# Spreading all parameter tables with TensorE in a conditional residual adapter with layer norm

## The chip, the cores and the metric

The kernel runs on one core of a Trainium2 chip. The core has five engines that run at the same time and wait for each other through semaphores: TensorE (PE, matrix products and transposes into PSUM), VectorE (DVE), ScalarE (ACT), GpSimd (POOL) and SyncE (SP, which here only issues transfers). Weight loads of TensorE are shown as an engine of their own, PEld. Transfers between device memory and the on-chip memory (SBUF) run on sixteen DMA engines.

The metric is the device time of one execution in microseconds (us). Beside it the profile has the span, from the first to the last instruction of one profiled execution.

## The reference

There are 128 batch rows, each a matrix of 128 positions by 512 features, and ten languages. Every batch row has a language, and with it weights and parameters of its own:

```
w1 = W1[language_ids]                       # 512 x 128 for each batch row
w2 = W2[language_ids]                       # 128 x 512
h = relu(einsum('bsh,bha->bsa', x, w1) + b1[language_ids])
adapted = einsum('bsa,bah->bsh', h, w2) + b2[language_ids]
y = x + adapted
normed = (y - mean(y)) * rsqrt(var(y) + 1e-5)
out = x + normed * gamma[language_ids] + beta[language_ids]
```

Mean and variance are taken over the 512 features. All is in float32. The output is 128 x 128 x 512.

## The kernel before

**Tiling.** One batch row is one tile of 128 positions (partitions) by 512 features. Below, "row b" is a batch row, and "row r" or "spread row" is a row of a parameter table. Rows of x come in groups of four (`load_x`, 1 MB; the first twelve rows as pairs, `load_part`), and results leave in pairs (`store`). The language of a row is a number in a register (`lid`), by which the tables are sliced as the kernel runs.

**One row's way.** `transpose_x` turns the four 128 x 128 blocks of x (TensorE, line 238), `copy_xT` takes them out of PSUM (ScalarE, L242), `down` multiplies by W1 (four products, each in two passes, L261), `relu` adds b1 (ScalarE, L269), `up` multiplies by W2 into a PSUM tile `py` (L278). For rows 0 to 3, and for one row in four or eight later, `up` first adds b2 with a product of its own (L277). For the others GpSimd adds b2 to x (`add_b2`, L248), or VectorE does (L291). `residual` (VectorE, L293) adds x or that sum and takes the row sums; `square` (ScalarE, L308), `deviation` and `rstd_1` to `rstd_4` make the reciprocal deviation; `scale` (VectorE, L342) multiplies by gamma; GpSimd has meanwhile made x + beta (`add_beta`, L255); `finish` (VectorE, L351) puts both together and frees the PSUM tile. Five PSUM tiles are shared by all `py` and by the spread rows (pool `p_y`); transposes and products down have one each (`p_x`, `p_h`).

**Order.** The order on every engine is the order of writing: `keep` ties each instruction to the one before it on its engine. The loop over `i` (line 506) runs the stages of several rows, shifted: in step i TensorE transposes row i, multiplies row i - 1 down and row i - 2 up, while VectorE works on row b = i - 3 and older ones. The last five rows have a schedule of their own (`tail`).

**Weights.** The first eight rows have W1 of their language loaded for them alone (`load_first`, tiles `w1s`, five buffers, so that the load for row 5 waits for `down(0)`). From row 8 on ScalarE copies a language's W1 out of a table of all ten (`stage_w1`, L229), at the end of step i for row i + 1, ahead of `copy_xT(i + 1)`. There are two tables. `w1e` is loaded early and used up to `EARLY`; its lines are split over the partitions as `(p k)`, so that x is transposed from every fourth column. `w1` is loaded in four parts within the loop (`load_w1`) and used from row `EARLY` on, with x transposed from neighbouring columns. W2 for all languages is one tile, which every `up` slices by language.

**Parameter tables.** gamma, beta and b2 have ten rows of 512 each, and every partition needs a copy. `rows` holds all thirty rows on partitions of their own; `parts` holds them as three bfloat16 parts, and a product with a column of `pick` spreads one row over the 128 partitions in PSUM (`spread`, L210), from where VectorE or ScalarE copies it into the table (L215, L213). The twenty rows of beta and gamma go this way, in turns between the first products. b2 is loaded a second time as one long line on one partition, into the memory of `w1`, and GpSimd spreads it with three broadcasts (L204):

```
b2_row = w1.rearrange("p l k a -> p (l k a)")[0:1, :]
keep(nc.gpsimd.partition_broadcast(b2_b[:, span], b2_row[:, span]))
```

**Transfers.** All large transfers are issued by SP, in the order of writing: ids, gamma, x of rows 0 and 1, two languages of W2, W1 for rows 0 and 1, x of rows 2 and 3, W1 for rows 2 and 3, the other eight languages of W2 as two transfers, then x and W1 for rows 4 to 7, x of rows 8 and 9, `w1e` in two halves, x of rows 10 and 11. In the loop follow stores, groups of x and the four parts of `w1` (steps 8, 10, 12 and 14). A transfer that has to wait holds up those behind it on SP. ScalarE's queue issues beta, b2, b1 and the b2 line.

The warm-up `spin(11, H)` runs eleven idle products on TensorE first.

Of the kernel before, what the change touches and what calls it, by code (L numbers as in the profile page):

```python
# [17 lines left out]
G = 4  # L18
EPS = 1e-5
FIRST = 8  # L20
EARLY = 28
U = 2


# [1 line left out]
def cond_resid_kernel(ctx: ExitStack, tc: tile.TileContext, x, itok, W1, b1, W2, b2, gamma, beta, out):  # L26
# [8 lines left out]
    nc = tc.nc  # L35
    B, S, H = x.shape
    L, _, A = W1.shape
# [7 lines left out]
    def keep(ins):  # L45

        engine = ins.ins.engine
        if engine in last:
            tc.add_manual_dep(ins.ins, last[engine], behind, reason="kept order")
        last[engine] = ins.ins.name  # L50
        return ins
# [15 lines left out]
    def load_x(g):  # L67
        t = xp.tile([P, G, H], FP, tag="x", name=f"x_{g}")
        keep(nc.sync.dma_start(out=t, in_=x[g * G : (g + 1) * G].rearrange("b s h -> s b h")))
        xs[g] = t  # L70

    def xb(b):
        return xs[b // G][:, b % G, :]
# [5 lines left out]
    w1 = const.tile([P, L, KC, A], FP, name="w1")  # L79
# [13 lines left out]
    load_part(0, 2)  # L93
    keep(nc.scalar.dma_start(out=b1r, in_=b1))

    b2_row = w1.rearrange("p l k a -> p (l k a)")[0:1, :]
    keep(nc.scalar.dma_start(out=b2_row, in_=b2.rearrange("(o l) h -> o (l h)", o=1)))

    warm = const.tile([P, 1], FP, name="warm")
    keep(nc.vector.memset(warm, 1.0))  # L100
    keep(nc.scalar.activation(warm, warm, AF.Sqrt))
    def load_w1(k):
        keep(
            nc.sync.dma_start(out=w1[:, :, k, :], in_=W1[:, k * P : (k + 1) * P, :].rearrange("l p a -> p l a"))
        )
# [10 lines left out]
    R = 3 * L  # L116
# [17 lines left out]
    def lid(b, engine):  # L134
        g = b // G
        if (g, engine) not in lids:
            loads, vals = nc.values_load_multi_w_load_instructions(
                lang[0:1, g * G : (g + 1) * G],
                engines=[engine],
                min_val=0,  # L140
                max_val=L - 1,
                skip_runtime_bounds_check_because="clamped on the chip to 0..L-1 above",
            )
            for ins in loads:
                keep(ins)
            lids[g, engine] = vals
        return lids[g, engine][b % G]
# [4 lines left out]
    def load_first(b):  # L152
        w1s[b] = wp.tile([P, KC, A], FP, tag="w1s", name=f"w1s_{b}")
        src = W1[bass.ds(lid(b, ET.SP), 1)].rearrange("o (p k) a -> p (o k a)", k=KC)
        keep(nc.sync.dma_start(out=w1s[b].rearrange("p k a -> p (k a)"), in_=src))  # L155

    def load_w2(lo, hi):
        dst = w2[:, lo * H : hi * H].rearrange("p (l h) -> p l h", l=hi - lo)
        keep(nc.sync.dma_start(out=dst, in_=W2[lo:hi].rearrange("l a h -> a l h")))  # L159
# [2 lines left out]
        dst = w1e[:, lo:hi].rearrange("p l k a -> p l (k a)")  # L162
        keep(nc.sync.dma_start(out=dst, in_=W1[lo:hi].rearrange("l (p k) a -> p l (k a)", k=KC)))

    load_w2(0, 2)
    load_first(0)
    load_first(1)
    load_part(2, G)
    load_first(2)
    load_first(3)  # L170
    load_w2(2, 6)
    load_w2(6, L)
    xs[1] = xp.tile([P, G, H], FP, tag="x", name="x_1")
    for b in (G, G + 2):
        load_part(b, b + 2)
# [23 lines left out]
    beta_b = const.tile([P, L * H], FP, name="beta_b")  # L199
    gamma_b = const.tile([P, L * H], FP, name="gamma_b")  # L200
    b2_b = const.tile([P, L * H], FP, name="b2_b")
    for l in range(0, L, 4):
        span = slice(l * H, min(l + 4, L) * H)
        keep(nc.gpsimd.partition_broadcast(b2_b[:, span], b2_row[:, span]))  # L204

    def spread(r, copier):
        t = (beta_b, gamma_b)[r // L]
        row = p_y.tile([P, H], FP, tag="y", name=f"row_{r}")
        pick_r = pick[:, r : r + 1].to_broadcast([96, P])
        keep(nc.tensor.matmul(row, lhsT=pick_r, rhs=parts[:96, :], start=True, stop=True))  # L210
        dst = t[:, r % L * H : (r % L + 1) * H]
        if copier is nc.scalar:
            keep(nc.scalar.copy(dst, row))  # L213
        else:
            keep(nc.vector.tensor_copy(dst, row))  # L215
# [10 lines left out]
    def stage_w1(b):  # L226
        w1s[b] = wp.tile([P, KC, A], FP, tag="w1s", name=f"w1s_{b}")
        src = (w1e if b < EARLY else w1).rearrange("p l k a -> p (l k a)")[:, bass.ds(lid(b, ET.Activation) * (KC * A), KC * A)]
        keep(nc.scalar.copy(w1s[b].rearrange("p k a -> p (k a)"), src))  # L229

    def transpose_x(b):
        pxs[b] = p_x.tile([P, KC, P], FP, tag="xT", name=f"pxT_{b}")
        for k in range(KC):
            if b < EARLY:
                cols = xb(b).rearrange("s (p k) -> s k p", k=KC)[:, k, :]
            else:
                cols = xb(b)[:, k * P : (k + 1) * P]
            keep(nc.tensor.transpose(pxs[b][:, k, :], cols, ident))  # L238

    def copy_xT(b):  # L240
        xT[b] = tp.tile([P, KC, P], FP, tag="xT", name=f"xT_{b}")
        keep(nc.scalar.copy(xT[b], pxs.pop(b)))  # L242
# [14 lines left out]
    def down(b):  # L257
        phs[b] = p_h.tile([P, P], FP, tag="h", name=f"ph_{b}")
        for k in range(KC):
            keep(  # L260
                nc.tensor.matmul(  # L261
                    phs[b], lhsT=w1s[b][:, k, :], rhs=xT[b][:, k, :], start=(k == 0), stop=(k == KC - 1)
                )
            )
        del xT[b], w1s[b]

    def relu(b):
        hT[b] = tp.tile([P, P], FP, tag="hT", name=f"hT_{b}", bufs=6)
        keep(nc.scalar.activation(hT[b], phs.pop(b), AF.Relu, bias=b1T[:, bass.ds(lid(b, ET.Activation), 1)]))  # L269

    def up(b):
        v = lid(b, ET.PE)
        ys[b] = p_y.tile([P, H], FP, tag="y", name=f"py_{b}")
        m = b2_by_matmul(b)
        if m:
            pick_b = pick[:, bass.ds(v + 2 * L, 1)].to_broadcast([96, P])
            keep(nc.tensor.matmul(ys[b], lhsT=pick_b, rhs=parts[:96, :], start=True, stop=False))  # L277
        keep(nc.tensor.matmul(ys[b], lhsT=hT[b], rhs=w2[:, bass.ds(v * H, H)], start=not m, stop=True))  # L278
        del hT[b]
# [78 lines left out]
    def on(b):  # L358
        return 0 <= b < B
# [122 lines left out]

    def spread_turn(lo, hi):
        for r in range(lo, hi):
            spread(r, nc.scalar if r % 3 == 1 else nc.vector)

    spread_turn(0, 2)
    transpose_x(0)
    transpose_b1()
    copy_xT(0)  # L490
    spread_turn(2, 6)
    transpose_x(1)
    copy_xT(1)
    spread_turn(6, 10)
    for b in range(4):
        down(b)
        if b < 2:
            transpose_x(b + 2)
        relu(b)
        if b < 2:  # L500
            copy_xT(b + 2)
        spread_turn((10, 14, 18, 20)[b], (14, 18, 20, 20)[b])
    up(0)
    up(1)

    for i in range(3, B + U):
        b = i - U - 1
        if b > G and b % G == 2 and b // G + 3 < NG:
            load_x(b // G + 3)
        if i == 5:  # L510
            load_x(3)
        if i in (8, 10, 12, 14):
            load_w1((i - 8) // 2)
        if i == 4:
            up(2)
        if i == 5:
            up(3)
        if i > 3 and on(i):
            transpose_x(i)
        if b <= E:  # L520
            add_b2(b + 2)
            add_beta(b)
        if i > 4 and on(i - 1):
            down(i - 1)
        if i > 3 and on(i):
            copy_xT(i)
        if i > 4 and on(i - 1):
            relu(i - 1)
        if i > 5 and on(i - U):
            up(i - U)  # L530


        g, half = divmod(b, 2)
        p = g - 1
        mine, old = 0 <= p < B // 2, 0 <= p - 1 < B // 2
        if b == E:
            add_b2(b + 3)
            add_beta(b + 1)
            add_b2(b + 4)
            for n in range(b + 2, B):  # L540
                add_beta(n)
        if b > E:
            tail(b)
        elif half == 0:
            if on(b):
                residual(b)
            if mine:
                rstd_1(p)
                scale(2 * p)
            if on(b):  # L550
                negative_mean(b)
            if mine:
                rstd_2(p)
            if old:
                finish(2 * p - 1)
                store(p - 1)
            if mine:
                rstd_3(p)
        else:
            if on(b):  # L560
                residual(b)
            if mine:
                rstd_4(p)
                scale(2 * p + 1)
            if on(b):
                negative_mean(b)
            if mine:
                finish(2 * p)
        if 0 <= b <= E:
            square(b)  # L570
            if half == 1:
                deviation(g)
        if i + 1 >= FIRST and on(i + 1):
            stage_w1(i + 1)

        for n, engine in ((i + 3, ET.Activation), (i - U + 3, ET.PE), (b + 1, ET.DVE), (b + 5, ET.Pool)):
            if on(n):
                lid(n, engine)
# [37 lines left out]
```

## Time and profile before

| what | value |
|---|---|
| median of three runs | 312.70 us (312.29 to 314.03) |
| profiled execution | 312.74 us |
| its span | 311.0 us |
| mean granted clock of TensorE | 0.989 of full speed |
| TensorE busy | 297.9 us, 96% |
| VectorE busy | 294.7 us, 95% |
| GpSimd busy | 285.4 us, 92% |
| ScalarE busy | 277.8 us, 89% |
| mean transfer rate | 250 GB/s over the span, 218 to 388 GB/s in the first six of forty slices |
| three broadcasts (L204), recorded | 5.6 us, from 10.65 us on |
| one `add_beta` / `add_b2` (L255 / L248), recorded mean | 1.29 us |

Busy shares are averages over the whole span. A TensorE product's end is modelled in the record, so its engine is read here by the starts of successive instructions. Spans on GpSimd are rough in the record. A releaser in brackets is inferred from semaphore events: it is the event that came last before an instruction started.

### The profile page before, as it was taken

What the parts mean: (1) busy time and instruction counts of PE and PEld (TensorE: products, weight loads), DVE (VectorE), ACT (ScalarE), POOL (GpSimd) and SP (SyncE); (2) the same over time, 40 slices, a digit from 0 to 9 for tenths busy, and PEclk for the clock granted to TensorE, in tenths of its full rate; (3) what the DMA queues carried; (4) which work ended last, traced back from release to release, by engine and by line L of the source; (5) the groups of instructions that cost most, each with busy time, mean ns of one, the idle gap of its engine ahead of it and who ended that gap; (6) DMA issues with size and microseconds to landing.
All of it is one profiled execution on the core that took longest, in us unless ns stands there. A gap on an engine that the chain in (4) does not pass through costs nothing.

```text
span 311.0 us, 7063 instructions
## 1 busy us (share of the span) xinstructions
PE 297.9 (96%) x1846; PEld 223.1 (72%) x1846; DVE 294.7 (95%) x941; ACT 277.8 (89%) x710; POOL 285.4 (92%) x237
## 2 busy tenths in 40 slices
PE   8998899999999999999999999999999999999970
PEld 3766677878777777777777777777777777777740
DVE  6845999999999999999999999999999999999995
ACT  2655899999999999999999999999999999999982
POOL 1606999999999999999999999999999999999974
PEclk9999999999999999999999999999999999999995
DMA  6999999876777757677866766577765767773234
GB/s 218 346 387 388 373 368 349 295 263 210 269 271 238 233 192 245 231 237 254 270 245 211 232 201 265 209 266 271 249 227 194 245 233 239 245 270 135 87 154 169
DMA packets 43499, 77.61 MB, mean 250 GB/s; under 512 B 1946, under 2 KB 7077, under 8 KB 43459
## 3 DMA queue, kind: packets, MB, share of 16 engines
q1 hardware_dynamic: 43398, 77.10, 71.8%
q8 instruction: 15, 0.25, 0.3%
q14 instruction: 24, 0.20, 0.2%
q10 hardware_dynamic: 62, 0.07, 0.1%
HBM read 43.60 MB, written 33.55 MB: 248 GB/s over the span
## 4 chain that ended last, share of the span: by engine, by line
PE 83%; DMA 8%; DVE 4%; SPq 1%; issue 1%; ACT 1%; DVEq 1%; POOL 0%; ACTq 0%; POOLq 0%
PE ph L261 33%; PE py L278 32%; PE pxT L238 17%; DMA w1e<-in_L_cond_W_dram 4%; DMA x<-in_x_dram 3%; PE py L277 1%; DVE py L293 1%; DVE py L342 1%; DVE o L351 1%; SPq L155 1%; ACT sq L386 0%; SPq L87 0%; DVEq L611 0%; SPq L159 0%; ACT n L402 0%
## 5 line engine op out<-in xcount | busy, mean ns | idle before, releaser
L255 POOL TENSOR_TENSOR o<-x,beta_b 128x512 f32<-128x512 f32 x128 | 163.2, 1290 | 9.4 <-ACT hT L269 9.4
L261 PE MATMUL ph<-xT,w1s 128*128 128x128 f32 x1024 | 135.5, 275 | 0.0
L278 PE MATMUL py<-w,hT 128*128 x256 | 131.2, 594 | 1.4 <-DVE o L351 1.3
L261 PEld LDWEIGHTS ph<-xT,w1s 128*128 128x128 f32 x1024 | 125.0, 192 | 1.5 <-ACT hT L269 0.8
L248 POOL TENSOR_TENSOR r<-x,b_b 128x512 f32<-128x512 f32 x93 | 120.0, 1291 | 0.0
L238 PEld LDWEIGHTS pxT<-ident,x 128*128 128x128 f32 x512 | 67.4, 154 | 65.4 <-issue 47.3
L342 DVE SCALAR_TENSOR_TENSOR py<-py,nmean,gamma_b 128x512 f32<-128x512 f32 x126 | 93.3, 740 | 0.0
L351 DVE SCALAR_TENSOR_TENSOR o<-py,rstd,o 128x512 f32<-128x512 f32 x122 | 90.7, 744 | 1.4 <-POOL o L255 1.4
L308 ACT ACTIVATE sq<-py,sum 128x512 f32<-128x512 f32 x124 | 84.9, 685 | 4.3 <-DVE py L293 4.3
L238 PE MATMUL pxT<-ident,x 128*128 128x128 f32 x512 | 78.1, 275 | 0.5 <-ACT xT L242 0.5
L242 ACT COPY xT<-pxT 128x512 f32<-128x512 f32 x128 | 75.0, 586 | 1.7 <-PE pxT L238 1.6
L293 DVE SCALAR_TENSOR_TENSOR py<-py,r 128x512 f32<-128x512 f32 x93 | 64.4, 692 | 2.5 <-POOL r L248 1.7
L229 ACT COPY w1s<-w 128x512 f32 x100 | 61.2, 612 | 0.0
L269 ACT ACTIVATE hT<-ph,b1T 128x128 f32<-128x128 f32 x128 | 47.1, 368 | 11.2 <-PE ph L261 7.4
L278 PEld LDWEIGHTS py<-w,hT 128*128 128x128 f32 x256 | 40.4, 192 | 4.7 <-issue 1.7
L293 DVE SCALAR_TENSOR_TENSOR py<-py,x 128x512 f32<-128x512 f32 x35 | 24.3, 695 | 3.3 <-PE py L278 2.7
L308 ACT ACTIVATION_READ_ACCUMULATOR sq<-py,sum 128x1 f32 x124 | 25.2, 203 | 0.0
L319 ACT ACTIVATE sd<-ssq,eps 128x2 f32<-128x2 f32 x62 | 18.3, 296 | 2.1
L299 DVE TENSOR_SCALAR nmean<-sum 128x1 f32<-128x1 f32 x128 | 19.3, 150 | 0.1
L325 DVE RECIPROCAL stat<-sd 128x2 f32<-128x2 f32 x62 | 12.8, 207 | 1.3 <-ACT sd L319 1.3
L204 POOL PARTITION_BROADCAST b_b<-w x3 | 5.6, 1968 | 9.0 <-DVE beta_b L215 9.0
L229 ACT COPY w1s<-w1e 128x512 f32 x20 | 12.2, 612 | 1.3 <-DMA w1e<-in_L_cond_W_dram 1.2
(55 smaller groups left out, 119.7 us busy)
## 6 DMA issues: line engine op xcount, KB each, us to landing
out_dram<-o SPq DMA_DIRECT2D x61, 512.0 KB, 3.6
x<-in_x_dram SPq DMA_DIRECT2D x29, 1024.0 KB, 6.4
x<-in_x_dram SPq DMA_DIRECT2D x6, 512.0 KB, 7.0
w1e<-in_L_cond_W_dram SPq DMA_DIRECT2D x2, 1280.0 KB, 13.4
w<-in_L_cond_W_dram SPq DMA_DIRECT2D x4, 640.0 KB
w1s<-in_L_cond_W_dram SPq DMA_DIRECT2D x8, 256.0 KB, 6.2
w<-in_L_cond_W_dram SPq DMA_DIRECT2D x2, 1024.0 KB
out_dram<-o SPq DMA_DIRECT2D x6, 256.0 KB, 2.0
```

The lines of the kernel that those rows point to most:

```text
L229: keep(nc.scalar.copy(w1s[b].rearrange("p k a -> p (k a)"), src))
L238: keep(nc.tensor.transpose(pxs[b][:, k, :], cols, ident))
L242: keep(nc.scalar.copy(xT[b], pxs.pop(b)))
L248: keep(nc.gpsimd.tensor_tensor(rs[b], xb(b), b2_b[:, bass.ds(v * H, H)], ALU.add))
L255: keep(nc.gpsimd.tensor_tensor(os[g][:, j, :], xb(b), beta_b[:, bass.ds(v * H, H)], ALU.add))
L261: nc.tensor.matmul(phs[b], lhsT=w1s[b][:, k, :], rhs=xT[b][:, k, :], start=(k == 0), stop=(k == KC - 1))
L269: keep(nc.scalar.activation(hT[b], phs.pop(b), AF.Relu, bias=b1T[:, bass.ds(lid(b, ET.Activation), 1)]))
L278: keep(nc.tensor.matmul(ys[b], lhsT=hT[b], rhs=w2[:, bass.ds(v * H, H)], start=not m, stop=True))
L293: nc.vector.scalar_tensor_tensor(ys[b], ys[b], 1.0, r, ALU.mult, ALU.add, accum_out=col(sums, b))
L308: nc.scalar.activation(sq, ys[b], AF.Square, bias=col(sums, b), scale=-float(H), accum_out=col(ssqs, b))
L342: nc.vector.scalar_tensor_tensor(ys[b], ys[b], col(nmeans, b), gamma_b[:, bass.ds(v * H, H)], ALU.add, ALU.mult)
L351: nc.vector.scalar_tensor_tensor(o, ys.pop(b), rstds[g][:, j : j + 1], o, ALU.mult, ALU.add)
```

## The change

The ten rows of b2 are spread by TensorE like those of beta and gamma, so there are thirty rows. The second load of b2, its line in the memory of `w1` and the three broadcasts on GpSimd are gone. The spread rows take other turns between the first transposes and products down: all thirty, and all four products down, now come before the first product up, and the transposes of rows 2 and 3 come after `down(1)`. ScalarE copies three rows of every seven (13 of 30; before, 7 of 20), VectorE the others (17; before, 13).

The first transfer of W2 has three languages in place of two, and the other seven follow as one transfer. `EARLY` is 24 in place of 28, and the four parts of `w1` are issued in steps 12, 14, 16 and 18 in place of 8, 10, 12 and 14.

```diff
-EARLY = 28
+EARLY = 24
...
-    b2_row = w1.rearrange("p l k a -> p (l k a)")[0:1, :]
-    keep(nc.scalar.dma_start(out=b2_row, in_=b2.rearrange("(o l) h -> o (l h)", o=1)))
...
-    load_w2(0, 2)
+    load_w2(0, 3)
     load_first(0)
     load_first(1)
     load_part(2, G)
     load_first(2)
     load_first(3)
-    load_w2(2, 6)
-    load_w2(6, L)
+    load_w2(3, L)
...
-    for l in range(0, L, 4):
-        span = slice(l * H, min(l + 4, L) * H)
-        keep(nc.gpsimd.partition_broadcast(b2_b[:, span], b2_row[:, span]))
 
     def spread(r, copier):
-        t = (beta_b, gamma_b)[r // L]
+        t = (beta_b, gamma_b, b2_b)[r // L]
...
-            spread(r, nc.scalar if r % 3 == 1 else nc.vector)
+            spread(r, nc.scalar if r % 7 in (1, 3, 5) else nc.vector)
+
+    def x_turn(b):
+        transpose_x(b)
+        copy_xT(b)
 
     spread_turn(0, 2)
     transpose_x(0)
     transpose_b1()
     copy_xT(0)
     spread_turn(2, 6)
-    transpose_x(1)
-    copy_xT(1)
-    spread_turn(6, 10)
-    for b in range(4):
-        down(b)
-        if b < 2:
-            transpose_x(b + 2)
-        relu(b)
-        if b < 2:
-            copy_xT(b + 2)
-        spread_turn((10, 14, 18, 20)[b], (14, 18, 20, 20)[b])
+    x_turn(1)
+    spread_turn(6, 11)
+    down(0)
+    relu(0)
+    spread_turn(11, 15)
+    down(1)
+    relu(1)
+    x_turn(2)
+    spread_turn(15, 19)
+    x_turn(3)
+    down(2)
+    relu(2)
+    spread_turn(19, 24)
+    down(3)
+    relu(3)
+    spread_turn(24, R)
     up(0)
     up(1)
...
-        if i in (8, 10, 12, 14):
-            load_w1((i - 8) // 2)
+        if i in (12, 14, 16, 18):
+            load_w1((i - 12) // 2)
```

## The prediction

> **What bounds the kernel now.** I read four views, in this order: the busy sums and the forty slices of the page, the chain that ended last, the waits and order of time of each engine in the first 36 us, and the DMA rate in half-microsecond stretches.
>
> First the sums and the chain of waits (start in us, length in us, what). From 33.36 us on the chain is nothing but TensorE, always transpose, product down, product up; before that it is two transfers, one behind the other.
>
> ```profile
> PE 297.9 (96%) x1846; PEld 223.1 (72%) x1846; DVE 294.7 (95%) x941; ACT 277.8 (89%) x710; POOL 285.4 (92%) x237
> 8.18 10.55 DMA x<-in_x_dram
> 18.74 13.36 DMA w1e<-in_L_cond_W_dram
> 33.36 0.74 PE pxT L238 x4
> 34.10 0.89 PE ph L261 x8
> 34.99 0.86 PE py L278 x2
> 75.44 0.22 PE py L277
> 76.52 0.44 PE pxT L238 x4
> ```
>
> Each batch row costs TensorE 0.47 + 0.89 + 0.86 = 2.22 us up to 76 us and 0.44 + 0.89 + 0.86 = 2.19 after, when the transposed columns no longer lie strided (row 28 on, `EARLY`), plus 0.22 for each b2 product of line 277. The engine never waits between 33.36 us and the last rows. So whatever the change does, its price is read at one point: the start of the ninth row's transpose, T(9), at 33.36. What moves that start moves the end; what happens before it and leaves it alone costs nothing.
>
> Now the front, by engine (start, length, engine, line; in brackets the idle time before and what ended it).
>
> ```profile
> 10.65 5.64 POOL L204 PARTITION_BROADCAST b_b<-w  x3 [8.95 <-DVE beta_b L215]
> 25.69 2.50 POOL L255 TENSOR_TENSOR o<-x,beta_b 128x512 f32<-128x512 f32 x2 [9.39 <-ACT hT L269]
> 26.99 0.75 DVE L351 SCALAR_TENSOR_TENSOR o<-py,rstd,o 128x512 f32<-128x512 f32 x1 [1.40 <-POOL o L255]
> 27.79 0.38 PE L277 MATMUL py<-parts,pick 96*128 96x512 bf16 x1 [0.33 <-DVE o L351]
> 31.72 1.12 PE L278 MATMUL py<-w,hT 128*128 x2 [1.33 <-DVE o L351]
> 32.20 0.62 ACT L229 COPY w1s<-w1e 128x512 f32 x1 [1.18 <-DMA w1e<-in_L_cond_W_dram]
> 33.36 0.74 PE L238 MATMUL pxT<-ident,x 128*128 128x128 f32 x4 [0.52 <-ACT xT L242]
> ```
>
> The reader is to see two separate delays. GpSimd starts its first `add_beta` at 25.69; neither x_0 nor the beta table is that late (its last copy ran at about 11 us), so I take it that the broadcasts hold the engine until then, though their recorded spans end at 16.3. That lateness passes through VectorE's `finish` to TensorE's PSUM buffers: idle at 27.3 to 27.79 and 30.2 to 31.72. Second, w1e lands at 32.10; ScalarE has `stage_w1(8)` ahead of `copy_xT(8)` in its queue, so the copy starts at 32.72 and T(9) at 33.36, 1.26 after the landing, with TensorE idle from 32.58. The second delay ends last.
>
> The transfers run at their limit nearly from the start (us, then busy time of each engine, last the granted clock, DMA share, GB/s):
>
> ```profile
> 7.00:7.50 0.50, 0.50 (x5) 0.38 (x3) 0.20 (x1) 0.50 (x2) 0.00 (x0) 1.00 0.92 160
> 7.50:8.00 0.50, 0.50 (x4) 0.24 (x5) 0.20 (x2) 0.50 (x2) 0.00 (x0) 1.00 0.50 61
> 8.00:8.50 0.50, 0.50 (x4) 0.37 (x3) 0.50 (x1) 0.18 (x2) 0.00 (x0) 1.00 0.92 332
> 20.00:20.50 0.50, 0.50 (x2) 0.20 (x1) 0.35 (x1) 0.23 (x2) 0.00 (x0) 1.00 1.03 381
> ```
>
> **The change part by part.**
>
> *Ten rows more on TensorE.* A spread row costs 0.22 on TensorE (four rows start at 7.54, what follows them at 8.41). Work after the warm-up, from 5.85: first two rows 0.84, 28 rows x 0.2175 = 6.09, first transpose 0.69 and three at 0.47 = 1.41, the b1 transpose 0.16, four products down at 0.89 = 3.57; together 12.76, so `up(0)` starts at 18.61. It starts at 16.96 now. With the copies (next part) I get 18.72; the walk, each step after the one before it: row 10 at 9.75, `down(0)` 9.97, rows 11 to 14 10.86, `down(1)` 11.73, T(2) 12.62, rows 15 to 18 13.09, T(3) 13.96, `down(2)` 14.43, rows 19 to 23 15.32, `down(3)` 16.41, row 24 17.30. But now the first product up waits 0.28 beyond the 0.22 of its b2 row (16.96 to 17.46), because the last of W2 lands about 17.3; at 18.94 it has landed. Two ups then end at 18.72 + 2 x 1.08 = 20.88 against 19.47: TensorE is 1.41 late there.
>
> *Their copies.* Five PSUM buffers: row r waits for the copy of row r-5. VectorE takes 17 copies at 0.62 (three in 1.88) = 10.5 and b1T 0.15, from 6.51, so 17.2 at best; ScalarE 13 at 0.54 (two in 1.08) = 7.0, four xT at 0.55 and four relus at 0.35, 10.6 from 6.94, so 17.6 at best. Both are shorter than TensorE's 18.61. Walking the written order, I find one real hold: row 29 waits for row 24, whose copy stands behind `relu(3)` on ScalarE (17.84 to 18.43); and `up(0)` waits for row 25's, 18.56. Row 28's copy ends at 19.8, ahead of `residual(0)`, which must wait for its product anyway. Bounds: if the copies cost nothing extra, 0; if the ten extra rows went at one engine's pace, 10 x 0.62 = 6.2 in place of 2.17, so +4.0. I take 0.1, because 20 rows went through the same buffers at TensorE's pace with only 0.53 lost (16.96 - 5.85 = 11.11 against 10.58 of work).
>
> *No broadcast on GpSimd.* `add_beta(0)` can run at about 11. `add_b2(4)` waits for row 29 (19.8) and ends at 21.1; `residual(4)`, now kept until 29.45 by it, needs it at about 28. So the two idles of TensorE, 0.50 + 1.50, go. What is late next is w1e. Without any hold, TensorE's work from 19.47 to T(9) is 13.89 - 0.50 - 1.50 - 0.78 = 11.11, so T(9) could start at 20.88 + 11.11 = 31.99. It is held to 33.36 by w1e as now: 1.37 of cover for the ten rows. If that cover were gone (w1e early) the front would decide, and the gain ends there.
>
> [...]
>
> *Loads.* W2's third language (256 KB) comes ahead of the first W1 rows, which land later by 262 KB / 390 GB/s = 0.67; `down(0)` at 9.97 should still find them, since the queue ran empty at about 8.0. One W2 issue (0.5 us of SP) and one 20 KB row go. SP waits for `down(0)`, (1), (2) before the loads of W1 rows 5, 6, 7: by the walk +0.2, -0.5, 0.0; some 2.3 MB stand in the queue at 17.4 (issued 7.4 MB, moved 5.1), 6 us of work, so this is hidden. What counts is whether w1e lands earlier. The bytes ahead of it are the same, so at least 0; at most the whole dip of 7.0 to 8.0 (0.28 MB short of 390 GB/s, 0.72) and 0.05 for the b2 row: 0.77. I take 0.33, the idle DMA share of 7.0 to 8.5 (0.04 + 0.25 + 0.04), because w1e ends with the slowest of the engines and half were still busy in the dip. A late end has no row that speaks for it.
>
> *EARLY 24.* Rows 24 to 27 are transposed from unstrided columns: 4 x (0.47 - 0.44) = -0.12. They read w1, which is loaded four steps later: its last part is issued at about 55 in place of 46, and with 20.8 MB ahead of its end, 12.28 moved by 36 us and 360 GB/s it lands at 59.6. `stage_w1(24)` runs at 67.56; 8 us of cover. In the queue of SP the stores and x loads that stood behind the w1 loads at 32 to 46 us go earlier.
>
> *After T(9).* GpSimd's operations start 1.233 us apart, 14 in eight rows: 17.3 us against TensorE's 17.74, so it is not the bound and an earlier start buys nothing there. The end of the kernel is untouched: GpSimd waits 1.75 us for ScalarE at 300.04.
>
> Sum: -0.33 - 0.12 = -0.45; 312.74 (span 311.0 and 1.74 around it) becomes 312.29. The median of the runs, 312.70, is the same within 0.04; I say 312.3. Half a per cent, 1.6 us, is about what a measurement of this kernel can tell from no change.
>
> [...]
>
> **The rivals.**
>
> *The dip is filled wholly.* w1e lands 0.77 early: 312.74 - 0.77 - 0.12 = 311.85; if other low stretches go too (229 and 176 GB/s at 10.5 to 11.5), TensorE's own order is the floor: 33.36 - 31.99 = 1.37, 311.25. For it: the empty queue. Against: the DMA share of 0.92 in the same stretches.
>
> *The copies set the pace (slower).* ScalarE's queue has relus and xT copies between row copies, each waiting for TensorE, and TensorE waits for the rows behind them. Up to 1.37 us of such waiting is covered; 1.49 makes no gain; 3.05 costs half a per cent. At one engine's pace T(9) starts at 31.99 + 4.03 = 36.02: 312.74 + 2.66 - 0.12 = 315.3. For it: one copy, row 24's, already holds two steps in my walk. Against: the 0.53 above.
>
> *w1 comes late for row 24.* Each us after 67.5 costs one; at 70 us 312.74 + 2.5 = 315.2. Against: 8 us of cover.
>
> *The change doesn't free GpSimd.* If 25.69 was set by ScalarE's relu, as the releaser says, all of GpSimd moves with TensorE by 1.41: `finish(1)` ends at 31.66 + 1.41 = 33.07 and not at 31.66, `up(6)` takes 0.86 behind it, and T(9) starts at about 34.0: 312.74 + 0.64 - 0.12 = 313.3. Against: the first add needs no relu.
>
> **How the numbers follow.** Forecast 0.60 (its own range 311.9 to 312.8); dip filled 0.17; copies 0.12; w1 late 0.05; GpSimd not freed 0.06. Faster by over 0.5% (under 311.1) is only beyond the floor, with the scatter of the runs (0.4 below the median): 0.08. Slower by over 0.5% (above 314.3): half of the copies' case, most of w1's, a part of the last, 0.14. Same 0.78. The range, 311.1 to 314.0, leaves out about 0.07 below and 0.13 above.
>
> **What would show it.** Right: the first `add_beta` near 11 us; no wait of TensorE for `finish` before 32; `up(0)` at 18 to 19; ScalarE still waiting for w1e at `stage_w1(8)`; T(9) at 32.6 to 33.4 and no idle after. Wrong: TensorE waiting for row copies for over 2 us, T(9) after 34, ScalarE waiting for w1 at about 67, or a gain after T(9).

## The result and the profile after

| | before | after |
|---|---|---|
| median, 14 runs each | 312.81 us (312.29 to 314.03) | 311.92 us (311.77 to 312.10) |
| ratio, 95% interval | | 0.9963 (0.9951 to 0.9974) |
| profiled execution, its span | 312.74, 311.0 | 311.92, 310.1 |
| w1e lands | 32.10 | 31.18 |
| ninth transpose, T(9), starts | 33.36 | 32.45 |

By the ratio the kernel is faster by 0.37% (0.26 to 0.49%), which lies within the half per cent that was called no change; the interval keeps clear of no difference. The medians differ by less, 0.89 us or 0.28%: five of the 14 runs of before lie at 313.4 to 314.0, and none of after lies above 312.1. The forecast was 312.3.

The chain of waits of after has the same shape as before: two transfers, then TensorE (start, length, what).

```profile
6.81 10.80 DMA x<-in_x_dram
17.62 13.56 DMA w1e<-in_L_cond_W_dram
31.29 0.08 ACT w1s L222
31.81 0.59 ACT xT L235
32.45 0.74 PE pxT L231 x4
```

The start of the TensorE chain is 0.91 earlier than before. From there the chain runs as before: the product up that started at 75.50 starts at 74.46, 1.04 earlier, the last ones at 298.38 in place of 299.38. The 0.13 between 0.91 and 1.04 belongs to the four rows whose columns no longer lie strided: in the run below that has `EARLY` at 28, the same product starts 42.13 after T(9), in before 42.14, in after 42.01. The profiled time is 0.82 shorter and not 1.0.

The order of time of the engines in the front of after (start, length, engine, line, operation; in brackets the idle time before, and what ended it):

```profile
10.84 2.50 POOL L248 TENSOR_TENSOR o<-x,beta_b 128x512 f32<-128x512 f32 x2 [9.38 <-DVE beta_b L208]
18.87 0.38 PE L270 MATMUL py<-parts,pick 96*128 96x512 bf16 x1 [0.48 <-DVE b_b L208]
19.58 1.26 POOL L241 TENSOR_TENSOR r<-x,b_b 128x512 f32<-128x512 f32 x1 [6.24 <-DVE b_b L208]
28.93 0.38 PE L270 MATMUL py<-parts,pick 96*128 96x512 bf16 x1
31.29 0.62 ACT L222 COPY w1s<-w1e 128x512 f32 x1 [1.12 <-DMA w1e<-in_L_cond_W_dram]
31.37 1.02 PE L271 MATMUL py<-w,hT 128*128 x2
32.45 0.74 PE L231 MATMUL pxT<-ident,x 128*128 128x128 f32 x4
```

GpSimd starts its first `add_beta` at 10.84 and not at 25.69, and TensorE has no wait for `finish` any more (28.93 stood at 27.79 with one, 31.37 at 31.72). TensorE is late at the first product up: 18.87 against 16.96. It makes that good by the missing waits: `up(6)` ends at 32.23, 0.22 before the start of T(9). So ScalarE still waits for w1e and TensorE for ScalarE, but now by 0.22 where it was 0.78.

The transfers, in half microseconds (last the granted clock, the DMA share, GB/s). Of after:

```profile
7.00:7.50 0.50, 0.50 (x4) 0.24 (x5) 0.21 (x2) 0.50 (x2) 0.00 (x0) 1.00 1.07 410
7.50:8.00 0.50, 0.50 (x4) 0.36 (x3) 0.50 (x1) 0.41 (x2) 0.00 (x0) 1.00 1.02 369
11.00:11.50 0.50, 0.50 (x5) 0.47 (x4) 0.50 (x2) 0.50 (x1) 0.50 (x1) 1.00 0.94 369
11.50:12.00 0.50, 0.50 (x7) 0.50 (x7) 0.50 (x2) 0.07 (x1) 0.50 (x1) 1.00 1.02 397
```

And of before, in the second of its low stretches:

```profile
11.00:11.50 0.50, 0.50 (x5) 0.44 (x5) 0.50 (x2) 0.21 (x1) 0.50 (x1) 1.00 0.99 176
11.50:12.00 0.50, 0.50 (x4) 0.19 (x2) 0.16 (x2) 0.39 (x1) 0.50 (x1) 1.00 0.88 295
```

The low stretch at 7 to 8 us is closed, and so is most of the one at 10.5 to 12 (its first half microsecond still has 225 GB/s; before had 229). Summed up, 1.93 MB had moved by 8 us where it was 1.70, and 3.42 MB by 12 us where it was 2.96; a lead of some 0.43 MB is then kept. W1e is complete when 10.8 MB have moved in before, 10.9 in after.

One line of SP's queue differs early on, in before and in after:

```profile
4.73 1.34 SPq L87 DMA_DIRECT2D x<-in_x_dram  x1
```

```profile
4.78 0.42 SPq L87 DMA_DIRECT2D x<-in_x_dram  x1
```

The issue of x for rows 2 and 3 holds SP for 1.34 us in before, though nothing is shown to make it wait, and for 0.42 in after. What follows on SP is earlier by 0.8 to 0.9, and by 1.4 behind the W2 loads (8.18 against 6.81), since one W2 issue of about 0.5 us is gone.

### The profile page after: what moved, and what is told of

Same layout as the page of the kernel before. It is cut to its first block, busy times and chain, and to the rows that moved or that the text cites. A ratio compares the mean times of both kernels' runs of the same rounds, so it can differ in the third digit from the quotient of the medians.

```text
span 310.1 us, 7084 instructions
## 1 busy us (share of the span) xinstructions
PE 298.7 (96%) x1856; PEld 223.5 (72%) x1856; DVE 297.3 (96%) x945; ACT 280.3 (90%) x716; POOL 280.4 (90%) x234
## 4 chain that ended last, share of the span: by engine, by line
PE 83%; DMA 8%; DVE 4%; ACT 1%; issue 1%; SPq 1%; DVEq 1%; ACTq 0%
PE ph L254 33%; PE py L271 32%; PE pxT L231 17%; DMA w1e<-in_L_cond_W_dram 4%; DMA x<-in_x_dram 3%; PE py L270 1%; DVE py L286 1%; DVE py L335 1%; DVE o L344 1%; SPq L152 1%; DMA ids<-in_itok_B_dram 0%; ACT sq L379 0%; DVEq L613 0%; ACT n L395 0%; DVE o L406 0%
## 5 line engine op out<-in xcount | busy, mean ns | idle before, releaser
L231 PEld LDWEIGHTS pxT<-ident,x 128*128 128x128 f32 x512 | 66.7, 152 | 65.0 <-issue 46.4
L222 ACT COPY w1s<-w 128x512 f32 x104 | 63.6, 612 | 0.0
L286 DVE DVE_READ_ACCUMULATOR py<-py,r 128x1 f32 x93 | 13.5, 145 | 0.0
L222 ACT COPY w1s<-w1e 128x512 f32 x16 | 9.8, 611 | 1.1 <-DMA w1e<-in_L_cond_W_dram 1.1
```

The source lines that it names most:

```text
L286: nc.vector.scalar_tensor_tensor(ys[b], ys[b], 1.0, r, ALU.mult, ALU.add, accum_out=col(sums, b))
```

## The experiments

Theory A is that of the prediction: w1e's landing sets T(9), T(9) sets the end, and the ten rows are covered. What the first four runs ask is what made w1e land earlier: the third language of W2 (A), or the b2 line and the broadcasts (B). All ratios are to the kernel before, run beside each kernel; its medians lay at 312.9. Times of events, T(9) above all, are those of the one profiled execution of each kernel.

**The third language in the kernel before.**

```diff
-    load_w2(0, 2)
+    load_w2(0, 3)
...
-    load_w2(2, 6)
+    load_w2(3, 6)
```

> The kernel before with one edit: three languages of W2 ahead of the first W1 rows in place of two. Theory A, the third language closes the low stretch of the transfers at 7 to 8 us: w1e lands at 31.3 to 31.6 and not at 32.1; TensorE still waits for GpSimd, so the ninth transpose starts at 32.6 to 32.8; 0.6 to 0.8 us less than before, about 312.1. Rival B, the removed b2 line and its broadcasts caused the low stretches: w1e lands at 32.1, the issue of x rows 2 and 3 on SP still takes 1.3 us, the time is that of before, 312.8.

Measured: 312.28, ratio 0.9976 (0.9953 to 0.9999). w1e had landed by 31.4. TensorE now waits for GpSimd's lateness, as its own order of time shows:

```profile
28.28 0.38 PE L277 MATMUL py<-parts,pick 96*128 96x512 bf16 x1 [0.91 <-DVE o L351]
32.19 1.12 PE L278 MATMUL py<-w,hT 128*128 x2 [1.31 <-DVE o L351]
33.15 0.63 PE L238 MATMUL pxT<-ident,x 128*128 128x128 f32 x4
```

T(9) starts at 33.15, right behind `up(6)`. So the third language does bring w1e forward by at least 0.7 here. In this execution, which took 312.51, most of that is lost to GpSimd: T(9) is only 0.21 earlier than in before, and misses the expected 32.6 to 32.8. The median of the ten runs (311.65 to 313.67) is lower by 0.64, what theory A expected, so how much is lost in the others isn't shown. SP's hold of 0.9 us is still there, in the pair of W1 issues just before (1.75 in place of 0.91).

**The spreads alone.** The kernel after with the old loads.

```diff
-EARLY = 24
+EARLY = 28
...
-    load_w2(0, 3)
+    load_w2(0, 2)
...
-    load_w2(3, L)
+    load_w2(2, 6)
+    load_w2(6, L)
...
-        if i in (12, 14, 16, 18):
-            load_w1((i - 12) // 2)
+        if i in (8, 10, 12, 14):
+            load_w1((i - 8) // 2)
```

> The kernel after with the old order of loads: W2 as 2, 4 and 4 languages, EARLY 28, the parts of w1 in steps 8 to 14. So only the thirty spread rows and the gone broadcasts and b2 line are new. Theory A (third language): w1e lands at 32.0, the ninth transpose starts at 33.3, the time is that of before within 0.1, 312.7. Rival B (b2 line): w1e lands at 31.2, and the time is 312.05, that of after plus 0.13 for EARLY.

Measured: 312.44, ratio 0.9973 (0.9954 to 0.9992); w1e landed at 31.70, T(9) started at 32.96. That is between the two expectations: 0.4 of the 0.9 comes without any change in the order or size of SP's loads. SP's issue of x took 0.43 here.

**The b2 line back in the kernel after.**

```diff
+    b2_row = w1.rearrange("p l k a -> p (l k a)")[0:1, :]
+    keep(nc.scalar.dma_start(out=b2_row, in_=b2.rearrange("(o l) h -> o (l h)", o=1)))
```

> The kernel after with the second load of b2 put back on ScalarE's queue, one line of 20 KB on one partition, which nothing reads; no broadcasts. Theory A: no change, w1e at 31.2, 311.9. Rival B in the form that the transfer of the line slows the others: w1e at 31.7 to 32.1, the issue of x rows 2 and 3 takes 1.3 us again, 312.4 to 312.8. If the broadcasts themselves slowed the transfers, 311.9 too.

Measured: 311.77, ratio 0.9951 (0.9927 to 0.9974), T(9) at 32.41. The transfer of the line costs nothing that can be seen; SP's issue of x took 0.42.

**Two languages first in the kernel after.**

```diff
-    load_w2(0, 3)
+    load_w2(0, 2)
...
-    load_w2(3, L)
+    load_w2(2, L)
```

> The kernel after with two languages of W2 first and eight in one transfer later. Theory A: the low stretch at 7 to 8 us is back, w1e lands 0.5 to 0.9 later, 312.4 to 312.8. Rival B: w1e at 31.2, 311.9.

Measured: 312.09, ratio 0.9980 (0.9949 to 1.0011; one of ten runs lay at 315.8, with a clock of 0.989, the others at 311.85 to 312.5). w1e landed by 31.2, T(9) started at 32.39. So in the profiled execution, at 311.85 the fastest of the ten, the third language is not needed. The median lies 0.32 above that of the run with the b2 line back, which has the third language and ran on the same chip, so some of its worth may remain. This kernel differs from the spreads alone, where w1e landed at 31.70, in `EARLY`, in the steps of the w1 parts (no w1 load is issued before 31 us in either) and in one thing that comes ahead of w1e: the last eight languages of W2 are one issue on SP and not two. With it x of rows 4 and 5 is issued at 6.50 and not at 7.03, and 7 to 8 us carry 397 and 410 GB/s in place of 320 and 283. The gone issue is thus worth some 0.5 us of w1e's landing in these two executions; the medians differ by 0.35, of which `EARLY` is 0.13. Theory A had the effect right and the cause only half.

**A small broadcast in the kernel after.**

```diff
+    small = const.tile([P, P], FP, name="small")
+    keep(nc.gpsimd.partition_broadcast(small, ident[0:1, :]))
```

> The kernel after with one small broadcast on GpSimd put ahead of its first add_beta: the first line of the identity, 128 columns, into a tile that nothing reads. It brings GpSimd's broadcast code back, not the b2 line and not the 2.6 MB that the three broadcasts wrote. Theory C, formed on the four runs before this one: that the program holds a broadcast at all costs SP about 0.9 us in its issues between 3.8 and 6.1 us, and the low stretch at 7 to 8 us follows; w1e lands at 31.7 to 32.1 and the time is 312.4 to 312.8, with more scatter among the runs. Rival: the low stretches came from the writing of the broadcasts; then 311.9 and SP's issue of x rows 2 and 3 takes 0.42 us.

Measured: 312.01, ratio 0.9957 (0.9933 to 0.9982). Theory C fell: SP's issue took 0.42, w1e landed by 31.0. But GpSimd's order of time shows what a broadcast is:

```profile
1.41 0.30 POOL masks.py:199 TENSOR_SCALAR_AFFINE_SELECT ident<-ident 128x128 f32<-128x128 f32 x1 [0.29 <-POOL ones L109]
10.23 0.43 POOL L199 PARTITION_BROADCAST small<-ident  x1 [8.53 <-DVE beta_b L210]
21.87 2.50 POOL L250 TENSOR_TENSOR o<-x,beta_b 128x512 f32<-128x512 f32 x2 [11.21 <-ACT sq L303]
```

Its input is ready at 1.71 and nothing stands ahead of it on the engine, yet it is recorded at 10.23, and the next add follows at 21.87. With one broadcast of 128 columns GpSimd does nothing else for 20 us. T(9) started at 32.22, at once when `up(6)` ended: an add as late as 21.87 does no harm here.

**One broadcast of three in the kernel before.**

```diff
-    for l in range(0, L, 4):
+    keep(nc.gpsimd.memset(b2_b[:, 4 * H :], 0.0))
+    for l in range(0, 4, 4):
```

> The kernel before with the first of the three broadcasts alone (four languages); the b2 table of the other six is zero, so b2 is left out for them. The question is what holds GpSimd's first add_beta until 25.69. [...] The time stays at 312.8 within its scatter, since w1e still lands at 32.1.

Measured: the first `add_beta` at 23.95, 13.08 after the recorded start of the broadcast; with three it was 15.04 (25.69 - 10.65), with 128 columns 11.64 (21.87 - 10.23). Over 5120 - 128 columns that is 0.68 ns a column, and 11.55 us that do not depend on the size; by this line the 2048 columns would take 12.95. It is an estimate from one execution each: the run with the third language, with three broadcasts too, has 15.23 (26.19 - 10.96). Neither a pure rate by columns (0.4 of the 15.04 after 10.65, 16.67) nor a start set by ScalarE's relu, at about 25.7, met it. What comes ahead of the recorded start is not a fixed amount: 8.5 us with the small broadcast, 6.56 here, behind a memset that ended at 4.31.

The time, 314.36 (a single run), is another matter, and came of the memset in this edit. It kept GpSimd busy from 1.65 to 4.31, and VectorE's two small operations of that time took 2.17 and 2.14 us in place of 0.17 and 0.21:

```profile
2.17 2.17 DVE L123 TENSOR_SCALAR pick<-pick 96x10 bf16<-96x10 bf16 x1
2.25 2.14 DVE L129 TENSOR_SCALAR wrap<-ids 1x128 int32<-1x128 int32 x1
```

The loads behind them came 1.9 us late and w1e landed at 33.7; T(9) started at 34.99, 1.63 later than in before, as the whole time is 1.62 longer. TensorE idled for 1.64 us before its first row (7.68), and from 9.42 to 12.84, by the rows below (0.71 is 0.42 us at full clock, 0.58 is 0.16), its clock was halved (stretch, then busy times, last three: granted clock, DMA share, GB/s):

```profile
8.00:9.00 1.00, 1.00 (x8) 0.78 (x7) 0.76 (x2) 0.69 (x2) 0.00 (x0) 1.00 0.84 236
9.00:10.00 1.00, 1.00 (x5) 0.46 (x4) 0.84 (x3) 0.60 (x2) 0.00 (x0) 0.71 0.93 264
10.00:11.00 1.00, 1.00 (x6) 0.91 (x5) 1.00 (x2) 0.37 (x1) 0.14 (x1) 0.50 0.91 324
11.00:12.00 1.00, 1.00 (x4) 0.30 (x2) 0.65 (x2) 0.67 (x2) 1.00 (x1) 0.50 0.91 318
12.00:13.00 1.00, 1.00 (x5) 0.81 (x4) 0.84 (x3) 0.50 (x1) 1.00 (x1) 0.58 0.88 225
```

The mean clock of this execution is 0.985; that of the profiled execution of before is 0.989, with 1.00 in each hundred microseconds up to 300.

**Without the ten rows.**

```diff
-    b2_b = const.tile([P, L * H], FP, name="b2_b")
+    b2_b = beta_b
...
-        for r in range(lo, hi):
+        for r in range(lo, min(hi, 2 * L)):
```

> The kernel after without its ten last spread rows; add_b2 and VectorE read the beta table in their place, so the b2 table is left out. The question is what the ten rows cost. Theory A (covered by the wait for w1e): up(6) ends 2.2 us earlier, at about 30.1, and the ninth transpose still starts at 32.4: 311.7 to 311.9, at most 0.2 less. Rival D, TensorE's order is the bound: 2.2 less, 309.7.

Measured: T(9) at 32.43, after an idle time of TensorE that is 2.4 us longer; rival D fell.

```profile
28.98 1.02 PE L271 MATMUL py<-w,hT 128*128 x2
32.43 0.75 PE L231 MATMUL pxT<-ident,x 128*128 128x128 f32 x4 [2.42 <-ACT xT L235]
```

The ten runs fell into two groups: five at 311.81 to 312.08, as in after, with a mean granted clock of 0.990 to 0.993, and five at 313.21 to 313.83 with 0.985 to 0.987. Their median, 312.64 (ratio 0.9998, 0.9975 to 1.0021), lies between the groups and says little. So the ten rows cost nothing, and taking them away costs 1.4 us in half of the executions. The profiled execution is one of the first group.

**Ten rows more.**

```diff
     spread_turn(24, R)
+    spread_turn(20, R)
```

> The kernel after with the ten b2 rows spread a second time, ahead of the first product up: forty rows. The cover that is left is 0.2 us (up(6) ends at 32.23, the ninth transpose starts at 32.45). Theory A: ten rows x 0.2175 less 0.2 is 2.0 us more, 313.9. If the copies out of PSUM set the pace for these back-to-back rows, ten rows over two engines at 0.62 and 0.54 are 2.9 us, so up to 314.6; at one engine's pace 318.

Measured: 314.85, ratio 1.0058 (1.0033 to 1.0084). The first product up starts at 22.16 in place of 18.87 and T(9) at 35.52, right behind `up(6)`:

```profile
22.16 0.38 PE L270 MATMUL py<-parts,pick 96*128 96x512 bf16 x1 [0.45 <-DVE b_b L208]
35.52 0.63 PE L231 MATMUL pxT<-ident,x 128*128 128x128 f32 x4
```

Ten rows cost 3.29 us there, 0.33 each and not 0.22, so the copies out of PSUM set their pace; that is nearest to the second form of the expectation (2.9 at two engines), and what is over the cover reaches the end one to one: T(9) +3.07, time +2.9.

**Half a megabyte ahead of w1e.**

```diff
+    more = w1.rearrange("p l k a -> p (l k a)")[:, 0 : 2 * H].rearrange("p (b h) -> p b h", b=2)
+    keep(nc.sync.dma_start(out=more, in_=x[0:2].rearrange("b s h -> s b h")))
     load_early(0, 5)
```

> The kernel after with one transfer more on SP's queue ahead of w1e: x of rows 0 and 1 once more, 512 KB, into the memory of w1, which nothing reads there. Theory A (the end follows w1e one to one): 0.524 MB at 388 GB/s is 1.35 us, w1e lands at 32.5, the ninth transpose starts at 33.8, 313.25, and some runs are slower by a further 1.6, since TensorE then waits 1.5 us. Rival: TensorE's own order is the bound, 311.9.

Measured: 313.20, ratio 0.9998 (0.9980 to 1.0016), 1.28 more than after; ScalarE's copy of w1e started at 32.86 and T(9) at 34.02, each 1.57 later. The profiled execution is 1.47 longer, so the end follows w1e nearly one to one. The further 1.6 us that some runs were expected to lose did not come in ten runs, with an idle time of 1.8 us by the starts (`up(6)` at 31.36, 0.86 long, T(9) at 34.02):

```profile
34.02 0.75 PE L233 MATMUL pxT<-ident,x 128*128 128x128 f32 x4 [1.64 <-ACT xT L237]
```

**The first copy of w1e behind the transpose's copy.** In step 8, on ScalarE:

```diff
             copy_xT(i)
+        if i == FIRST:
+            stage_w1(i)
...
-        if i + 1 >= FIRST and on(i + 1):
+        if i + 1 > FIRST and on(i + 1):
```

> The kernel after with one move on ScalarE: the first stage_w1, of row 8, comes after copy_xT(8) and not ahead of it, so the ninth transpose no longer stands behind w1e. Theory A: w1e needs 0.7 us more until its copy is made (31.9), product down of row 8 wants it at 32.7; the ninth transpose starts when up(6) ends, 32.23 in place of 32.45: 311.7, 0.2 less than after. Rival, w1e binds through the product instead: no change, 311.9.

Measured: 311.58, ratio 0.9947 (0.9929 to 0.9965); nine of eleven runs at 311.53 to 311.79. T(9) starts when `up(6)` ends. The profiled execution is one of the two later ones, 312.29: the transfer of the table rows let `parts` begin at 3.87 and not at 3.08, so that TensorE's whole front came 0.8 late, and with no slack left that reached the end.

**The first product up earlier.** The last edit, and:

```diff
-    spread_turn(24, R)
-    up(0)
+    spread_turn(24, 27)
+    up(0)
+    spread_turn(27, R)
     up(1)
```

> The edit of the last plan (first stage_w1 after copy_xT(8)) and a second one: up(0) comes ahead of the last three spread rows, so that TensorE no longer waits 0.48 us for the copy of row 25 there. W2 landed at 16.2, ahead of it. Theory A: the ninth transpose at about 31.75, product down of row 8 at 32.2, the copy of w1e ready at 31.9: 311.2, 0.7 less than after. Rival: up(0) and up(1) now hold two of the five PSUM tiles while the last rows pass through the others, the wait comes back at rows 28 and 29, and the time is that of the last plan, 311.7.

Measured: 311.43, ratio 0.9949 (0.9924 to 0.9975), eleven of twelve runs at 310.98 to 311.85, one at 315.08 with a clock of 0.991; the median lies between the expected 311.2 and the rival's 311.7. TensorE's wait of 0.48 before `up(0)` is gone, T(9) starts at 31.53:

```profile
17.60 0.38 PE L270 MATMUL py<-parts,pick 96*128 96x512 bf16 x1
31.53 0.63 PE L231 MATMUL pxT<-ident,x 128*128 128x128 f32 x4
34.12 0.75 PE L231 MATMUL pxT<-ident,x 128*128 128x128 f32 x4
```

T(10), at 34.12, is 0.66 ahead of after's 34.78. Its median is the lowest of the kernels that compute everything, but 0.15 below the last plan's is within the scatter. After was not timed on the same chip, so the 0.5 between it and this kernel is a comparison of ratios, 0.9949 and 0.9963, whose intervals overlap.

**The idle time filled.** The kernel without the ten rows, with the product of `up(6)` made three times over, to see whether the second group goes when TensorE's idle time is filled:

```diff
-        keep(nc.tensor.matmul(ys[b], lhsT=hT[b], rhs=w2[:, bass.ds(v * H, H)], start=not m, stop=True))
+        for _ in range(3 if b == 6 else 1):
+            keep(nc.tensor.matmul(ys[b], lhsT=hT[b], rhs=w2[:, bass.ds(v * H, H)], start=not m, stop=True))
```

> The kernel without the ten b2 rows (five of its ten runs were 311.8 to 312.1, five 313.2 to 313.8, these with a mean clock of 0.985 to 0.987 and not 0.990 to 0.993), and up(6) makes its product three times over, each time from the start: 1.7 us more work for TensorE in the 2.4 us in which it waits for w1e. As there, the b2 table is left out. [...]

Measured: 311.87, ratio 0.9949 (0.9929 to 0.9969); ten runs at 311.51 to 312.06, all with a clock of 0.988 or more. With more work on TensorE the second group is gone, 0 of ten runs for five of ten, and the edit changes nothing else. So for that kernel the second group goes with TensorE's idle time. The two kernels ran on different chips, and no execution of the second group was profiled; that its clock was halved for a while is argued from its mean clock alone (0.985 to 0.987 and not 0.990 to 0.993), which is near the 0.985 of the run with one broadcast, where the trace shows the halving, and is not shown: a run of after at 311.84 has 0.987 too.

## Why the prediction was right, and where it was not

**The place and the bound: right.** "Its price is read at one point", T(9): 0.91 there and 0.13 from `EARLY` make up the 1.0 by which TensorE ends earlier, of which the profiled time keeps 0.82. Of the signs that were named, T(9) alone came a little outside, at 32.45 and not 32.6 to 33.4, since w1e was earlier still. The run with 512 KB more ahead of w1e shows that the end follows that transfer; the run without the ten rows shows that TensorE's own work did not decide.

**Ten rows and their copies: right, a little short.** `up(0)` at 18.72 was forecast and came at 18.87, held by row 25's copy as in the walk, for 0.48. `up(6)` ended at 32.23 where 31.99 was worked out as the earliest T(9), so the cover was 1.13 of the 1.37. The ten rows cost nothing in the end. Written back to back, beyond the cover, they would cost 0.33 each: the rival "the copies set the pace" has its mechanism and was 0.22 us away from counting.

**GpSimd: right.** The broadcasts did hold it: 10.84 for the forecast "about 11", and both idles of TensorE are gone. The forecast did not know that most of the price does not depend on the size: from the recorded start to the next add it was 11.64 us with 128 columns and 15.04 with 5120. In the run with the small one GpSimd did nothing but that broadcast, 0.43 us long in the record, from 1.71 to 21.87. What fills that time no run shows.

**Loads: the term that was mis-sized.** The forecast took 0.33 for w1e, with 0.77 as its upper bound; w1e landed 0.92 earlier. The step that failed is "at most the whole dip of 7.0 to 8.0": the second low stretch, at 10.5 to 12, was closed for the most part too, which only the rival "the dip is filled wholly" mentioned. Its figure for one stretch, 311.85, was nearest to what came, in part by luck: it had 0.77 for w1e where 0.92 came, and nothing for the 0.2 us of TensorE's gain that the time did not keep. The reason given for the small value, that half of the DMA engines were still busy in the dip, was wrong: the bytes moved by 8 us grew by 0.23 MB. That w1e ends with the slowest of the engines no run shows.

The cause given for it, the third language, was half right. In the kernel before it alone brings w1e to 31.4 or earlier; in the kernel after w1e is as early without it in the profiled execution, though the median there is 0.32 higher. W1e's landings are 32.10 in before, 31.70 with the spreads alone, by 31.2 with W2's rest in one issue, and 31.18 with the third language too. The forecast named the gone issue, "One W2 issue (0.5 us of SP)", and gave it no price of its own. What the profiled kernels with w1e at 31.4 or earlier have in common is a full queue from 7 to 9 us: 369 GB/s or more in every half microsecond of after and of the runs with the third language, with the b2 line, with two languages first and with the small broadcast, where before had 61 to 360 and the spreads alone 283 to 381. What of the 0.4 of the spreads alone comes from SP no longer being held is not shown. The hold itself, 0.9 us near 5 us on SP, stands in the two profiled kernels with all three broadcasts, and its cause stays open. The b2 line does not make it, nor does a small broadcast, nor one broadcast of three together with the b2 line (0.42, though SP is 1.9 us later there).

**The busiest engine.** TensorE was busiest over the span, 297.9 us or 96%, and got ten products more. Counted in full they would have made 312.74 + 2.17 - 0.12 = 314.8, an estimate from 0.2175 a row and the 0.12 of `EARLY`; 311.92 was measured. Between the rows and T(9) TensorE waited 2.8 us in before (0.50, 1.50 and 0.78), which a share of the span does not show.

**What the forecast had no term for.** Of the runs of before with a recorded clock, 22 of 88 lie at 314.1 us or more with a mean clock of 0.984 to 0.987; the 14 runs of after all lie within 0.33 us. In before TensorE idles 1.5 and then 0.78 us between 30.2 and 33.4. That its second group too goes with the idle time is argued from the same clock and a like size, 1.6 us against 1.4, and not shown; before itself was not run with its idle time filled. If it is so, the change also takes away a chance of one in four of 1.6 us, which a median hardly shows and the ratio does.

## What to carry to other kernels

Price an addition at the point where the waits end: ten more products on the busiest engine cost nothing here, because they stood in its wait for a transfer, and the worth of that wait was 1.1 us, no more. Count issues as well as bytes ahead of a transfer that others wait for: one issue of 0.5 us less on SP went with a landing of w1e some 0.5 us earlier. Where two delays end close together, removing one alone can be worth less: in the profiled executions the earlier transfers gave 0.2 at T(9) while GpSimd was late, and 0.9 with it out of the way, though the medians show a smaller difference (0.64 and 0.89). Where TensorE idles for some two microseconds ahead of a long run of products, try filling the time and look at the single runs and not only at the median: with 2.6 us of it here five runs of ten took 1.4 us more, with the time filled none of ten. Do not call GpSimd's broadcast for a table while a short product can spread it and TensorE has the time: three broadcasts held GpSimd for 15.04 us from their recorded start to the next add, where ten products took 0.22 us each and no time in the end.

## What the hardware showed that was not expected

- Broadcasts on GpSimd had a price that hardly depended on their size: 11.64, 13.08 and 15.04 us from the recorded start to the next add for 128, 2048 and 5120 columns, one execution each (by an estimate from the first and the last 11.55 us and 0.68 ns a column), and in the run with the small one 8.5 us more before its recorded start.
- TensorE's clock fell to 0.50 for 3.4 us (9.42 to 12.84), some 1.7 us after the end of an idle time of 1.64 us, in the run with one broadcast. In the kernel without the ten rows, some 2.6 us of waiting before T(9) went with a lower mean clock (0.985 to 0.987 and not 0.990 to 0.993) and 1.4 us more in five executions of ten; 1.8 us, in the run with 512 KB more, cost none in ten. Why only some executions are slower is not shown.
- Beside a memset of 2.66 us on GpSimd two operations of VectorE, 0.17 and 0.21 us long otherwise, took 2.17 and 2.14 us, until 4.34 and 4.39, just behind its end at 4.31, in one execution.
